# A hybrid block on one core: two feed-forward slices of ten chunks run during the last two chunks, the last chunk's state sums moved from TensorE to GpSimd, B and C computed in column tiles, state copies on ScalarE and state adds on VectorE

## The chip, the cores and the metric

The kernel runs on one core of one Trainium2 chip. The metric is the device time of one execution in microseconds (us), median over the runs. The engines are TensorE (PE, its weight loads PEld), VectorE (DVE), ScalarE (ACT), GpSimd (POOL) and SyncE (SP), which here issues nearly all DMAs.

## The reference, cut to what matters

A block of four residual layers over x of shape (2, 2048, 512), all in float32: an RWKV attention, a feed-forward layer, a Mamba layer and the same feed-forward layer again.

```python
def ffn(x, lut, gate_idx, up_idx, down_idx):       # weights are table entries
    gate = einsum('bsh,oh->bso', x, lut[gate_idx])     # 512 -> 1376
    up   = einsum('bsh,oh->bso', x, lut[up_idx])
    return einsum('bsh,oh->bso', silu(gate) * up, lut[down_idx])   # 1376 -> 512

def mamba(x):                                      # inner width 1024, 16 states
    xs, gate = split(x @ in_proj)                      # 512 -> 2 x 1024
    u = silu(causal_conv4(xs) + conv_b)
    dt_lr, B, C = split(u @ x_proj)                    # 128, 16 and 16 columns
    delta = softplus(dt_lr @ dt_proj + dt_proj_b)
    for t in range(2048):                              # h starts at 0 for each sequence
        h = h * exp(delta[t] * A) + (delta[t] * u[t]) * B[t]     # 1024 x 16 states
        y[t] = sum_n(h * C[t])
    return ((y + u * D) * silu(gate)) @ out_proj

x = x + rwkv(layernorm(x)); x = x + ffn(layernorm(x))
x = x + mamba(layernorm(x)); x = x + ffn(layernorm(x))
```

## The kernel before, in words

The 4096 tokens run in two stages. The first stage (up to about 700 us) is the RWKV layer in eight chunks of 512 tokens. Beside it the 11 slices of feed-forward weights (128 of the 1376 inner columns each, the last has 96) are looked up and written to DRAM as `wff[0..10]`. The second stage does the rest in 16 chunks of 256 tokens, chunks 0 to 7 of one sequence and 8 to 15 of the other.

The second stage is written as a list of steps, each with a time in slots: `line.at(t, fn)` (L52) notes a step, `emit` sorts all steps by time, and the steps are issued in this order. The times therefore only set the order in which each engine's instructions stand. A window has 32 slots, and window `w` starts at `t = 32 * w`. The dictionary `AT` (L538) holds the offsets. In window `w` stand

- the state scan of chunk `w` (`scan`, L819): for each of 2 halves, 4 groups of states `q` and 4 column blocks `c4` POOL computes `du * B` (`grow`, L844) and adds the carried state to the first token (L847); ACT computes the decays (`decay`, L854) for two states at a time into one of three PSUM tiles; DVE runs the scan (L864), multiplies by C (L865) and copies the last token's state to `hst` (L869); POOL adds up the states (`fold`, L876 to L882). That is 32 steps of POOL and 64 of DVE for each chunk;
- the out-projection (`project`) and the second feed-forward layer of chunk `w - 1`, whose result is stored to `out`;
- the front of chunk `w + 1` (`front`, L709): layer norm, in-projection, convolution, and `x_product` (L757), which makes the step sizes and B and C; B and C go to DRAM as `bcd` and come back spread over the partitions (L827);
- the first feed-forward layer of chunk `w + 2`.

So window 14 has no first feed-forward layer, window 15 no front either, and after window 15 only the last chunk's out-projection and second feed-forward layer are left. In the last chunk POOL's `fold` is not used: `spread` (L884) sums the states on PE with matmuls against the identity (L890).

`feed_forward` (L655) takes the slices in pairs, six times `pairs` 0, 2, 4, 6, 8 and the single slice 10: gate and up products (L666), silu on ACT (L684), product on DVE (L693), and at the end the down products of all slices into two PSUM banks (`residual`, L643), which DVE adds to x (L647). The weights come through a `Stream` of 18 buffers of 256 KB, issued by SP in the order of use. PSUM has five banks for all products (`mmp`) and three for the decays (`dap`).

Of the kernel before, what the change touches and what calls it, by code (L numbers as in the profile page):

```python
# [44 lines left out]
class Line:  # L45
# [9 lines left out]
    def emit(self):  # L55
        for _, _, fn, args in sorted(self.items, key=lambda item: item[:2]):
            fn(*args)


@with_exitstack  # L60
def block_kernel(ctx: ExitStack, tc: tile.TileContext, a: dict, out: bass.AP):
# [33 lines left out]
    with ExitStack() as pa:  # L95
# [26 lines left out]
        AA = dict(k=-1.307, r=-0.678, v=-0.887, head=-1.102, sig=-0.532, top=-0.981, e1=-0.692,  # L122
                  e2=-0.655, state=-0.546, vb=-0.433, car=-0.292, num=0.236, den=-0.252, rec=0.174,
                  y=0.611, x=-3.627, stats=-3.064, stat=0.11, each=0.083, copy=0.089, fmul=0.602,
                  opened=-2.211, mean=-2.385, scale=-2.198, turn=-2.092, out=3.908, outs=0.06,
                  add=0.062, looks=(1.565, 14.126), ahead=0.368, load=2.503, cast=1.5, deal=1.4,
                  take=0.479, ff=(14.55, 31.36), place=-8.33, ffln=10.812, nextln=8.791, flast=1.322,
                  turned=1.577, fgate=0.448, fdown=2.092, times=0.273)
# [378 lines left out]
    with ExitStack() as pb:  # L507
        NWS, LEAD = 18, 8.0
        wpool = pb.enter_context(tc.tile_pool(name="b_w", bufs=1))
        xp = pb.enter_context(tc.tile_pool(name="b_x", bufs=8))  # L510
# [16 lines left out]
        wdt = wpool.tile([P, DI], F32, name="wdt")  # L527

        def load_w():
# [8 lines left out]
        AT = dict(total=-0.417, y=1.456, decay=1.1, grow=1.63, fold=2.892, gates=(2.59, 0.82,  # L538
                  24.962, 26.99), front=(6.05, 6.48, 7.41, 8.16), f2=(8.75, 8.93, 12.67, 14.17, 14.38,
                  16.88), f1=(22.279, 21.331, 24.749, 26.059, 30.199, 26.446), f2d=16.9, f1d=30.14,  # L540
                  x=11.293, step0=20.687, step1=10.517, step=0.088, soft=0.09, du=2.158, carry=2.337,
                  zero=3.0, proj=2.49, frontln=3.04, f2ln=5.981, f1ln=18.923, store=29.713, taps=1.14,
                  conv=0.04, unit=1.885, add=0.6, silu=-0.29, hT=0.409, scale=0.19, turn=0.82,
                  g1ln=-4.921, g1=-0.28, g1s=1.491, late=8.031, step1a=-5.78, ahead=12.53, spread=2.23,
                  gsilu=0.359, bca=1.408, step0a=23.69, fronta=(-0.27, 2.4, 1.42, 4.191), xa=14.67)
# [44 lines left out]
        def store_x(ci):  # L590
            for j in range(NJ):
                r = ci * TB + j * P
                nc.sync.dma_start(out[r : r + P, :], xs[ci][j])
            del xs[ci]

        def ln(t, ci, box, to=None):


            def stats():
                box["xnT"] = to if to is not None else tp.tile([P, KC, TB], F32, tag="xnT", name="xnT")  # L600
                st = small.tile([P, NJ, 6], F32, tag="st", name="st")
                mv = small.tile([P, NJ, 2], F32, tag="mv", name="mv")
                rs = small.tile([P, NJ, 1], F32, tag="rs", name="rs")
                for j in range(NJ):
                    V.bn_stats(st[:, j, :], xs[ci][j])  # L605
                    V.bn_aggr(mv[:, j, :], st[:, j, :])
                G.tensor_scalar(rs, mv[:, :, 1:2], EPS, None, ALU.add)
                G.tensor_tensor(rs[:, :, 0], rs[:, :, 0], mhalf[:, :NJ], ALU.pow)  # L608
                nrs = small.tile([P, NJ, 1], F32, tag="nrs", name="nrs")
                G.tensor_scalar(nrs, rs, -1.0, None, ALU.mult)  # L610
                box["mv"], box["rs"], box["nrs"] = mv, rs, nrs

            def scale(j):
                box["xn", j] = wk.tile([P, C], F32, tag="xn", name="xn")
                nm = small.tile([P, 1], F32, tag=f"nm{j}", name="nm")
                S.activation(nm, box["mv"][:, j, 0:1], AF.Copy, scale=box["nrs"][:, j, :])
                S.activation(box["xn", j], xs[ci][j], AF.Identity, bias=nm, scale=box["rs"][:, j, :])  # L617

            def turn(j):
                tr = mmp.tile([P, KC, P], F32, tag="mm", name="tr")  # L620
                for k in range(KC):
                    PE.transpose(tr[:, k, :], box["xn", j][:, k * P : (k + 1) * P], ident)  # L622
                S.copy(box["xnT"][:, :, j * P : (j + 1) * P], tr)  # L623

            line.at(t, stats)
            for j in range(NJ):
                line.at(t + AT["scale"] + 0.1 * j, scale, j)
                line.at(t + AT["turn"] + 0.1 * j, turn, j)

# [25 lines left out]
        def feed_forward(t_ln, times, td, dtd, ci, layer=1):  # L655

            box, hT, ps = {}, {}, {}
            if ci == 1 and layer == 0:
# [39 lines left out]
            for i, ti in zip(range(0, NF, 2), times):  # L698
# [8 lines left out]
            residual([td + dtd * i for i in range(NF)], ci, lambda i: hT[i], lambda i: wff[i][:, 2 * C :])  # L707

        def front(t_ln, times, tx, ci, box):  # L709
# [47 lines left out]
            def x_product():  # L757
                p2 = mm()
                for j, (lo, m) in enumerate(((0, RK), (RK, 2 * NS))):
                    for c in range(ND):  # L760
                        PE.matmul(p2[:m, j, :], lhsT=wxp[:, c, lo : lo + m], rhs=box["u"][:, c, :],
                                  start=(c == 0), stop=(c == ND - 1))
                bcs = wk.tile([2 * NS, TB], F32, tag="bcs", name="bcs", bufs=1)
                S.copy(bcs, p2[: 2 * NS, 1, :])
                box["dtl"] = wk.tile([P, TB], F32, tag="dtl", name="dtl")
                S.copy(box["dtl"], p2[:, 0, :])
# [3 lines left out]
            line.at(tx, x_product)  # L770

# [47 lines left out]
        def scan(t, gates, ci, box):  # L819
# [22 lines left out]
            def grow(half, q, c4):  # L842
# [3 lines left out]
                if ci % (SEQ // TB):  # L846
                    G.tensor_tensor(d[:, :, 0], d[:, :, 0],  # L847
                                    h0[:, 4 * half + c4, 4 * q : 4 * q + 4], ALU.add)
# [8 lines left out]
            def run(half, q, c4, m):  # L857
# [7 lines left out]
                V.tensor_tensor(d[:, two, :], h, cs[half, q][:, two, :], ALU.mult)  # L865
                c, col = 4 * half + c4, 4 * q + 2 * m

                if (ci + 1) % (SEQ // TB):
                    V.tensor_copy(hst[:, c, col : col + 2], h[:, :, TB - 1])  # L869

            def fold(half, q, c4):

                if ci == nchunk - 1:
                    return
# [19 lines left out]
            def total(cp):  # L894

                if ci == nchunk - 1:
                    return
# [5 lines left out]
            def close(cp):  # L903

                if ci == nchunk - 1:
# [9 lines left out]
            for half in range(2):  # L915
# [8 lines left out]
                for q in range(NQ):  # L924
                    line.at(th + 4 * q - 4.0 - AT["bca"] * (ci == 0 and half == 0 and q < 2), load, half, q)
                    for c4 in range(4):
                        s, k = th + 4 * q + c4, (half, q, c4)
                        line.at(s - AT["grow"], grow, *k)
                        for m in range(2):
                            line.at(s - AT["decay"] + 0.5 * m, decay, *k, m)  # L930
                            line.at(s + 0.5 * m, run, *k, m)
                        line.at(s + AT["fold"], fold, *k)
                        if ci == nchunk - 1:
# [10 lines left out]
        for w in range(-1, nchunk + 1):  # L944
            t = SLOTS * w
# [3 lines left out]
            if w > 0:  # L949
# [3 lines left out]
                feed_forward(t + AT["f2ln"], [t + f for f in AT["f2"]], t + AT["f2d"], 0.33, w - 1)  # L953
                line.at(t + AT["store"], store_x, w - 1)
# [13 lines left out]
            if w >= 0 and w + 2 < nchunk:  # L968
                line.at(t + 18.0, load_x, w + 2)
                feed_forward(t + AT["f1ln"], [t + f for f in AT["f1"]], t + AT["f1d"], 0.33, w + 2, layer=0)  # L970
        stream.lay()
# [60 lines left out]
```

## Time and profile before

| | us |
|---|---|
| median of 3 runs | 3535.88 (3534.11 to 3536.36) |
| the profiled execution's own time | 3528.32 |
| its span, first to last instruction | 3526.5 |
| first stage, up to the first scan | 708.5 |
| chunk 0 | 160.2 |
| chunks 1 to 13, each | 171.3 to 173.6 |
| chunk 14, chunk 15 | 165.6, 161.3 |
| after the last scan | 80.9 |

The lower rows are read from the times at which DVE starts the first scan (L864) of each chunk. Busy times overlap where an engine is pipelined, so what counts below is what an engine waits for: a stretch without its waits is what the engine itself needs. A float32 matmul shows as two records.

### The profile page before, as it was taken

What the parts mean: (1) busy time and instruction counts of PE and PEld (TensorE: products, weight loads), DVE (VectorE), ACT (ScalarE), POOL (GpSimd) and SP (SyncE); (2) the same over time, 40 slices, a digit from 0 to 9 for tenths busy, and PEclk for the clock granted to TensorE, in tenths of its full rate; (3) what the DMA queues carried; (4) which work ended last, traced back from release to release, by engine and by line L of the source; (5) the groups of instructions that cost most, each with busy time, mean ns of one, the idle gap of its engine ahead of it and who ended that gap; (6) DMA issues with size and microseconds to landing.
All of it is one profiled execution on the core that took longest, in us unless ns stands there. A gap on an engine that the chain in (4) does not pass through costs nothing. (4 is left out here: it accounts for less than half of the span.)

```text
span 3526.5 us, 45022 instructions
## 1 busy us (share of the span) xinstructions
PE 3355.6 (95%) x13744; PEld 2269.1 (64%) x13744; DVE 2891.1 (82%) x4522; ACT 2575.4 (73%) x4522; POOL 2807.6 (80%) x2755
## 2 busy tenths in 40 slices
PE   7999999889999999999999999999999999998698
PEld 3443555566777777777777777776767676765575
DVE  6777544399989898989898989898989898989882
ACT  6655867578878787878787878787878787877551
POOL 4344434298999999999999998999999999999840
PEclk9999999999999999999999999999999999999899
DMA  6553111365565656565656565656565656563442
GB/s 181 154 157 110 60 54 60 111 231 162 172 210 174 207 179 203 180 201 181 204 176 212 176 209 178 205 180 200 182 204 181 208 179 205 181 200 126 149 141 63
DMA packets 275505, 594.75 MB, mean 169 GB/s; under 512 B 31168, under 2 KB 32832, under 8 KB 275264
## 3 DMA queue, kind: packets, MB, share of 16 engines
q1 hardware_dynamic: 274464, 590.31, 53.4%
q8 instruction: 110, 1.80, 0.2%
q10 hardware_dynamic: 800, 1.57, 0.1%
q14 instruction: 131, 1.07, 0.1%
HBM read 560.96 MB, written 30.80 MB: 168 GB/s over the span
## 5 line engine op out<-in xcount | busy, mean ns | idle before, releaser
L864 DVE TENSOR_TENSOR_SCAN h<-h,db 128x512 f32<-128x512 f32 x1024 | 1252.2, 1223 | 98.5 <-ACT h L854 59.5
L844 POOL TENSOR_TENSOR db<-du,bc 128x1024 f32<-128x1024 f32 x512 | 1206.4, 2356 | 50.9 <-PE y L890 47.9
L854 ACT ACTIVATE h<-dl,acol 128x256 f32<-128x256 f32 x2048 | 952.3, 474 | 288.4 <-DVE hst L869 199.4
L865 DVE TENSOR_TENSOR db<-h,bc 128x512 f32<-128x512 f32 x1024 | 707.7, 691 | 35.9
L876 POOL TENSOR_TENSOR db<-db 128x512 f32<-128x512 f32 x480 | 609.3, 1269 | 0.0
L643 PE MATMUL po<-w,hT 128*128 128x512 f32 x1364 | 602.4, 592 | 0.0
L666 PE MATMUL pg<-xnT,w 128*128 128x256 f32 x2400 | 545.0, 381 | 1.6 <-ACT xnT L623 0.7
L666 PE MATMUL gu<-xnT,w 128*128 128x256 f32 x2400 | 541.0, 380 | 3.5 <-ACT hT L684 3.5
L666 PEld LDWEIGHTS pg<-xnT,w 128*128 128x128 f32 x2400 | 455.4, 191 | 80.4 <-issue 12.5
L666 PEld LDWEIGHTS gu<-xnT,w 128*128 128x128 f32 x2400 | 454.8, 190 | 76.8 <-ACT hT L684 9.1
L643 PEld LDWEIGHTS po<-w,hT 128*128 128x128 f32 x1364 | 258.1, 190 | 282.2 <-issue 266.3
L882 POOL TENSOR_TENSOR acc<-db 128x256 f32<-128x256 f32 x480 | 348.4, 726 | 37.6
L381 PE MATMUL ps<-xnT,wrvk 128*128 128x512 f32 x768 | 344.0, 597 | 0.7 <-ACT xnT L253 0.7
L854 ACT ACT_TABLE_LOAD x246 | 315.6, 1283 | 12.1 <-DVE hst L869 7.5
L381 PEld LDWEIGHTS ps<-xnT,wrvk 128*128 128x128 f32 x768 | 142.4, 190 | 175.6 <-issue 169.5
L834 PE MATMUL ps<-ready,w 128*128 128x256 f32 x1024 | 234.1, 382 | 9.8 <-DMA w<-in_in_proj 9.8
L721 PE MATMUL ps<-ready,w 128*128 128x256 f32 x1024 | 230.4, 384 | 9.2 <-DMA w<-in_in_proj 8.4
L643 PE MATMUL po<-w,u 128*128 128x512 f32 x512 | 229.4, 595 | 3.2 <-DVE u L913 3.2
L834 PEld LDWEIGHTS ps<-ready,w 128*128 128x128 f32 x1024 | 196.7, 192 | 50.6 <-ACT h L854 13.5
L721 PEld LDWEIGHTS ps<-ready,w 128*128 128x128 f32 x1024 | 196.4, 193 | 42.6 <-issue 14.6
L741 DVE SCALAR_TENSOR_TENSOR ps<-xin,cw,ps 128x256 f32<-128x256 f32 x384 | 185.8, 488 | 29.3 <-ACT ps L735 18.8
L443 POOL TENSOR_TENSOR d<-aa,opq 128x512 f32<-128x512 f32 x32 | 39.5, 1236 | 212.6 <-DVE opq L428 155.9
(144 smaller groups left out, 4307.8 us busy)
## 6 DMA issues: line engine op xcount, KB each, us to landing
w<-wff SPq DMA_DIRECT2D x1023, 256.0 KB, 2.7
bc<-bcd SPq DMA_DIRECT2D x256, 512.0 KB, 4.9
w<-in_in_proj SPq DMA_DIRECT2D x256, 256.0 KB, 2.9
w<-in_out_proj SPq DMA_DIRECT2D x128, 256.0 KB, 2.8
ixg<-ixd SPq DMA_DIRECT2D x44, 384.0 KB, 6.2
ix<-in_idx SPq DMA_DIRECT2D x11, 768.0 KB, 9.7
wff<-wt SPq DMA_DIRECT2D x11, 768.0 KB, 4.0
w<-wff SPq DMA_DIRECT2D x11, 768.0 KB, 4.2
```

The lines of the kernel that those rows point to most:

```text
L381: PE.matmul(ps, lhsT=wrvk[:, k, lo : lo + P], rhs=chunk["xnT"][:, k, :], start=(k == 0), stop=(k == KC - 1))
L643: PE.matmul(po[j], lhsT=lw[:, j * P : (j + 1) * P], rhs=w[i]["w"][:m], start=(i == 0), stop=(i == n - 1))
L666: PE.matmul(to[:m], lhsT=w[:, k, :m], rhs=box["xnT"][:, k, :], start=(k == 0), stop=(k == KC - 1))
L721: PE.matmul(ps[cp][:, j, :], lhsT=wj[:, k, :], rhs=box["xnT"][:, k, :], start=(k == 0), stop=(k == KC - 1))
L741: V.scalar_tensor_tensor(ps[cp][:, j, :], xin[cp][:, j, i : i + TB], cw[:, c, i : i + 1], ps[cp][:, j, :], ALU.mult, ALU.add)
L834: PE.matmul(ps[:, j, :], lhsT=wj[:, k, :], rhs=box["xnT"][:, k, :], start=(k == 0), stop=(k == KC - 1))
L844: G.tensor_tensor(d, box["du", half][:, c4, :].unsqueeze(1).to_broadcast([P, 4, TB]), bs[half, q], ALU.mult)
L854: S.activation(h[:, n, :], box["dl", half][:, c4, :], AF.Exp, scale=acol[:, 4 * half + c4, col : col + 1])
L864: V.tensor_tensor_scan(flat(h), flat(h), flat(d[:, two, :]), 0.0, ALU.mult, ALU.add)
L865: V.tensor_tensor(d[:, two, :], h, cs[half, q][:, two, :], ALU.mult)
L876: G.tensor_tensor(d[:, 0:2, :], d[:, 0:2, :], d[:, 2:4, :], ALU.add)
L882: G.tensor_tensor(to, d[:, 0, :], d[:, 1, :], ALU.add)
```

## The change

- **Later slices.** For chunks 2 to 11 (`LATER`) the second feed-forward layer leaves out the pair of slices 8 and 9. The normalised input is written to DRAM (`keep_x`, 512 KB), and x goes to DRAM in place of `out`. Ten steps `rest`, all noted in window 14 with times in windows 14, 15 and 16 (three, six and one), read both back (`fetch_x`), run slices 8 and 9, add, and store to `out`.
- **No identity sums.** `fold`, `total` and `close` test for chunk `nchunk`, which never comes, in place of `nchunk - 1`: the last chunk is summed on POOL like the others.
- **B and C in column tiles.** The eight 32-column products of `x_product` are dealt to four groups of 32 columns, their sum over the four groups is copied from PSUM by ACT, and one matmul with `sum4` (four identities of 32 stacked) adds the groups up (`rates_product`), some 2.8 slots later; only then `bcd` is written.
- **State copies and adds.** The copy to `hst` moves from DVE to ACT (`keep`), 0.27 slots after its scan; the add of the carried state moves from POOL to DVE (`enter`), 0.73 slots ahead of its scan.
- **Order.** `AA` and `AT` have new numbers, and `SHIFT` adds to them in windows -1, 0, 14, 15 and 16. Pools: x tiles 8 to 10, `xnT` 2 to 3.

```diff
-        xp = pb.enter_context(tc.tile_pool(name="b_x", bufs=8))
+        xp = pb.enter_context(tc.tile_pool(name="b_x", bufs=10))
...
+        LATER = range(2, 2 + len(AT["rest"]))
...
+        def keep_x(ci, box):
+            nc.sync.dma_start(xnd[ci], box["xnT"])
+
+        def fetch_x(ci, box):
+            box["xnT"] = tp.tile([P, KC, TB], F32, tag="xnT", name="xnT", bufs=3)
+            nc.sync.dma_start(box["xnT"], xnd[ci])
+            xs[ci] = []
+            for j in range(NJ):
+                x2 = xp.tile([P, C], F32, tag="x", name="x")
+                nc.sync.dma_start(x2, x2d[ci][j * P : (j + 1) * P, :])
+                xs[ci].append(x2)
+
+        def rest(ci, t):
+            box = {}
+            line.at(t - AT["fetch"], fetch_x, ci, box)
+            feed_forward(None, [t], t + AT["restd"], 0.33, ci, pairs=[8], given=box)
+            line.at(t + AT["restd"] + 2.0, store_x, ci)
...
             def x_product():
-                p2 = mm()
-                for j, (lo, m) in enumerate(((0, RK), (RK, 2 * NS))):
-                    for c in range(ND):
-                        PE.matmul(p2[:m, j, :], lhsT=wxp[:, c, lo : lo + m], rhs=box["u"][:, c, :],
-                                  start=(c == 0), stop=(c == ND - 1))
+                p2 = box["p2"] = mm()
+                for c in range(ND):
+                    PE.matmul(p2[:, 0, :], lhsT=wxp[:, c, :RK], rhs=box["u"][:, c, :],
+                              start=(c == 0), stop=(c == ND - 1))
+                for c in range(ND):
+                    g = slice(c % 4 * 2 * NS, (c % 4 + 1) * 2 * NS)
+                    PE.matmul(p2[g, 1, :], lhsT=wxp[:, c, RK:], rhs=box["u"][:, c, :],
+                              start=(c < 4), stop=(c >= 4))
+                parts = box["parts"] = wk.tile([P, TB], F32, tag="parts", name="parts", bufs=1)
+                S.copy(parts, p2[:, 1, :])
+                box["dtl"] = wk.tile([P, TB], F32, tag="dtl", name="dtl")
+                S.copy(box["dtl"], p2[:, 0, :])
+
+            def rates_product():
+                p2 = box["p2"]
+                PE.matmul(p2[: 2 * NS, 1, :], lhsT=sum4, rhs=box["parts"], start=True, stop=True)
                 bcs = wk.tile([2 * NS, TB], F32, tag="bcs", name="bcs", bufs=1)
                 S.copy(bcs, p2[: 2 * NS, 1, :])
...
             line.at(tx, x_product)
+            line.at(tx + AT["rates"], rates_product)
...
-                if ci % (SEQ // TB):
-                    G.tensor_tensor(d[:, :, 0], d[:, :, 0],
-                                    h0[:, 4 * half + c4, 4 * q : 4 * q + 4], ALU.add)
+
+            def enter(half, q, c4):
+                d = db[half, q, c4]
+                V.tensor_tensor(d[:, :, 0], d[:, :, 0],
+                                h0[:, 4 * half + c4, 4 * q : 4 * q + 4], ALU.add)
...
+            def keep(half, q, c4, m):
                 c, col = 4 * half + c4, 4 * q + 2 * m
-
-                if (ci + 1) % (SEQ // TB):
-                    V.tensor_copy(hst[:, c, col : col + 2], h[:, :, TB - 1])
+                S.copy(hst[:, c, col : col + 2], db[half, q, c4, m][:, :, TB - 1])
...
             def fold(half, q, c4):
-                if ci == nchunk - 1:
+                if ci == nchunk:
                     return
...
                         line.at(s - AT["grow"], grow, *k)
+                        if ci % (SEQ // TB):
+                            line.at(s - AT["enter"], enter, *k)
                         for m in range(2):
                             line.at(s - AT["decay"] + 0.5 * m, decay, *k, m)
                             line.at(s + 0.5 * m, run, *k, m)
+                            if (ci + 1) % (SEQ // TB):
+                                line.at(s + 0.5 * m + AT["keep"], keep, *k, m)
...
+                some = w - 1 in LATER
+                pairs = [i for i in range(0, NF, 2) if not (some and i == 8)]
+                box = feed_forward(t + AT["f2ln"], [t + AT["f2"][i // 2] for i in pairs], t + AT["f2d"], 0.33,
+                                   w - 1, pairs=pairs)
+                if some:
+                    line.at(t + AT["f2ln"] + AT["turn"] + 0.4, keep_x, w - 1, box)
+                line.at(t + AT["store"], store_x, w - 1, x2d[w - 1] if some else None)
...
+            if w == nchunk - 2:
+                for ci, r in zip(LATER, AT["rest"]):
+                    rest(ci, t + r)
```

## The prediction

> **What bounds the kernel now.** First the page's busy times, then each engine's waits over chunks 2 to 12, then single stretches.
>
> ```profile
> PE 3355.6 (95%) x13744; PEld 2269.1 (64%) x13744; DVE 2891.1 (82%) x4522; ACT 2575.4 (73%) x4522; POOL 2807.6 (80%) x2755
> ```
>
> PE looks like the bound, but 80% for POOL is a mean with the first stage, where it is half idle. The waits between 1042 and 2945 us (11 chunks), for PE, POOL and the longest of DVE and ACT:
>
> ```profile
> PE ps L761 <- DVE hT L693: 16.2, 11, 1.5
> PE tr L622 <- ACT xn L617: 14.7, 26, 1.0
> POOL rs L607 <- DVE mv L606: 31.3, 13, 5.6
> DVE hT L696 <- PE ps L666: 55.2, 11, 5.5
> ACT h L854 <- DVE hst L869: 129.9, 159, 1.9
> ```
>
> In these 1903 us PE waited 34 us and POOL 33 (3 each per chunk of 173), DVE 147 (13.4 per chunk), ACT 368 (33.5). PE and POOL are both full; relieving PE alone would give 3 us per chunk. The next two views tell what POOL needs without L847: chunks 5, 8, 14 and 15 from the first `grow` on (busy PE, PEld, DVE, ACT, POOL, then clock), and POOL in chunks 7 and 8.
>
> ```profile
> 1556.50:1729.90 173.40, 169.84 (x674) 122.75 (x672) 156.31 (x259) 135.91 (x245) 163.74 (x166) 1.00 0.62 192
> 2075.80:2245.60 169.80, 167.40 (x663) 120.83 (x662) 153.61 (x251) 134.67 (x242) 157.81 (x134) 1.00 0.62 190
> 3112.40:3281.60 169.20, 132.69 (x498) 92.08 (x496) 155.66 (x255) 125.18 (x231) 162.42 (x163) 0.92 0.47 151
> 3281.60:3433.50 151.90, 142.43 (x552) 105.78 (x553) 122.43 (x146) 90.22 (x163) 95.45 (x85) 0.96 0.46 152
> ```
>
> ```profile
> 1799.28 2.35 POOL L844 TENSOR_TENSOR db<-du,bc 128x1024 f32<-128x1024 f32 x1
> 1801.71 0.20 POOL L847 TENSOR_TENSOR db<-db,h 128x4 f32<-128x4 f32 x1
> 1801.86 1.28 POOL L876 TENSOR_TENSOR db<-db 128x512 f32<-128x512 f32 x1
> 1803.21 0.72 POOL L882 TENSOR_TENSOR acc<-db 128x256 f32<-128x256 f32 x1
> 1803.90 2.35 POOL L844 TENSOR_TENSOR db<-du,bc 128x1024 f32<-128x1024 f32 x1
> ...
> 2106.53 2.36 POOL L844 TENSOR_TENSOR db<-du,bc 128x1024 f32<-128x1024 f32 x1
> 2108.84 1.27 POOL L876 TENSOR_TENSOR db<-db 128x512 f32<-128x512 f32 x1
> 2110.20 0.73 POOL L882 TENSOR_TENSOR acc<-db 128x256 f32<-128x256 f32 x1
> 2110.88 2.35 POOL L844 TENSOR_TENSOR db<-du,bc 128x1024 f32<-128x1024 f32 x1
> ```
>
> Chunk 8 starts a sequence and has no L847: one step takes 4.35 us against 4.62. In chunk 14 POOL waited for nothing, though PE had 36 us free: POOL alone sets 169.2 us there. In chunk 15 PE has its identity sums. Last the end, where PE waits for the layer norm:
>
> ```profile
> 3448.06:3455.20 7.14, 7.13 (x16) 2.96 (x16) 2.21 (x4) 0.00 (x0) 0.00 (x0) 1.00 0.33 94
> 3455.20:3460.19 4.99, 0.00 (x0) 0.00 (x0) 2.23 (x5) 1.16 (x3) 1.17 (x3) 0.77 0.22 75
> 3460.19:3463.00 2.81, 2.15 (x8) 1.43 (x8) 0.00 (x0) 2.14 (x5) 0.00 (x0) 0.50 0.00 0
> 3463.00:3467.00 4.00, 3.98 (x9) 3.17 (x10) 0.00 (x0) 1.26 (x1) 0.00 (x0) 0.50 0.00 0
> ```
>
> Five idle us bring the granted clock to 0.50; the transposes take 2.15 us where eight take 1.0 in the first stage, and the first 32 records 9.5 us up to the next group instead of 6.9.
>
> **The change, part by part.** *Later slices.* Records of 256 columns follow each other at 0.216 us, of 512 at 0.430. A pair is 32 gate and up records (6.9 us) and 8 down records (3.4): 10.35 us of PE, 103.5 for ten. ACT loses a silu (0.60) and two table loads (1.28 each), DVE a product (0.7). SP issues six 256 KB loads less and a 512 KB store more; the store waits for ACT's copy of `xnT`, and the weight loads queue behind it. The queue already stands so at L768 (118 us over the 11 chunks, up to 10.8 at once) while 18 buffers hold some 33 us of work, and PE's list shows no wait for weights. Cost nothing; without that cover, up to 10 us per chunk.
>
> *L847 to DVE.* POOL: 32 times 0.27, 8.6 us less per chunk. On DVE the nearest row is L114 (128x4, 0.16 us); followed by something independent such operations pass in 0.07 us, followed by a dependent one in 0.20: 2.2 to 6.4 us, I take 4. It waits for `grow`, with one scan queued behind it, whose own data are ready. POOL's `fold` that uses this scan comes nearly four steps (17 us) later in POOL's order, so nobody late waits for it.
>
> *hst copies to ACT.* DVE's next instruction starts 0.07 us after a copy: 64 copies, 4.5 us less (by the 0.149 of the row, 9.5). On ACT the nearest row is L732 (0.196 us, next start after 0.10): 6.4 to 12.6 us; I take 10. The copy waits for its scan, and queued behind it are the decays for the third tile ahead, which need the same tile's release anyway, and any silu that stands between. Between the two I take the upper half, since a copy that has waited cannot start behind its forerunner at 0.10.
>
> *B and C.* Before: 16 records at 0.216, 3.46 us. In the first stage four records of 32 columns run side by side (24 of L201 in 1.41 us with the change of shape, 0.1). If all four do so here: 0.86 + 0.43 for `sum4` + 0.2 for one more change of shape there and back, 2.0 us less; if none do, 0.6 us more. The two records of one float32 matmul go to the same columns and stand next to each other, so I reckon with two side by side: 0.9 us less. The Trainium skill (TensorE: Matmul & The Clock Gate, Part 3) speaks against the full gain: weight loads overlap running matmuls only in another row group, and three column tiles gave 2.38 times; by that 1.4 us less here. The PSUM bank of `p2` is held 2.8 slots longer, one of five; I take nothing, at worst a pair waits 2 us per chunk.
>
> *No identity sums.* In chunk 15 PE loses 256 records (55 us), POOL gains 32 folds: 32 x (1.34 + 0.68) + 16 x 0.81 = 77.6 us.
>
> *Sum by stage.* POOL in the ten chunks 3 to 12: 173.4 - 2.7 (its wait) - 8.6 = 162.1 us; chunk 8 confirms it with 169.8 less 7.4 of waits, 162.4. PE: 169.8 - 10.35 - 0.9 = 158.6. DVE: 173.4 - 13.4 - 4.5 - 0.7 + 4 = 158.8. ACT: 173.4 - 33.5 - 3.2 + 0.3 + 10 = 147. POOL is the bound; with the loss of 2.9 us that the two full engines show now, 165 us.
> - Chunks 3 to 12: 1729.8 us from first scan to first scan become 1650: -79.8.
> - Chunks 1, 2 and 13 keep PE as bound: 3 x -0.9 = -2.7.
> - Chunk 14: POOL 169.2 - 8.6 = 160.6, PE 132.7 + 3 x 10.35 - 0.9 = 162.8, some of it at the clock of 0.92 that fills up; 163.4: -5.8.
> - Chunk 15: from first `grow` to the last gating, 166.4 us before. POOL: 151.9 - 53.1 idle + 77.6 - 8.6 = 167.8, then one add and the product on DVE, 1.5: +2.9. PE: 142.4 - 55.3 + 62.1 = 149, beside it.
> - End: the pair in the gap. Out-projection to the end of the first 32 records 17.3 us; then 6.9 + 1.0 + 3.4 + 6.9 = 18.2: +0.9, as the clock stays up; +4.8 if it does not.
> - Start of the second stage: twelve weight loads stand on SP between `bcd` and the first B and C (7.3 us, L827 at 699.9), afterwards six, and two more ahead of `bcd`; four less at 0.6 us: -2.4. First stage and chunk 0, reordered: 0, from -8 to +8 (PE waits some 18 us there after its first product).
>
> Together -87: 3526.5 becomes 3439.5. The median stands 9.4 us above that span: 3449.
>
> **Rivals.** *ACT and DVE pace it.* Four engines are left between 147 and 162 us, and DVE waits 4 us per chunk for decays already. If half of DVE's 13.4 us stays, and its waits for decays double by 4 us since ACT stands at copies, the ten chunks take 158.8 + 6.7 + 4 = 170. Then -30 with nothing from the other terms, median 3506. For it: in-order queues bound to each other by three tiles. Against it: PE and POOL, equally full, lose only 3 us.
> *POOL without loss, and retuned order pays*: 162.1, and -8 in the first stage: -29 and -8 more, 3412.
> *Slower: copies hold up ACT.* A copy stands at 0.69 of the space between two decays (0.267 + 1.077 - 1.0 of 0.5 slots), so a third of ACT's some 20 other steps per chunk (silu, softplus, convolution) fall behind one. If each then loses a DVE tile (1.26 + 0.69 us), that is 12 us per chunk behind POOL's 165: 177 in ten chunks (+40), and some 8 more in each of chunks 1, 2, 13, 14 and 15, where PE or POOL hide a third of it (+40): 3616. It decides from about 6 us per chunk on, where 15 chunks lose the 87 again, 9 if DVE's 3 us of slack under POOL take the first part. Against it: ACT waits 12 us per chunk for the same DVE tiles now.
> *Column tiles do not overlap*: +1.5 us in four chunks, hidden by POOL in the ten: 3455, inside the range.
>
> **How the numbers follow.** POOL-bound with a small loss 0.68, paced by ACT and DVE 0.14, without loss 0.08, held up 0.08, all else 0.02. The range reaches to 3414 (no loss) and 3508 (paced), and leaves out the held-up case. A measurement of this kernel can tell about 0.2% from no change (7 us); -87 and -30 are clear of it. Faster 0.90, same 0.02, slower 0.08.
>
> **What would show it.** Right: chunks 3 to 12 take 163 to 167 us between first scans, POOL's waits there stay under 4 us per chunk, PE's grow to 6; L847's successor is short on DVE; chunk 15 has no PE in its sums and POOL full; no clock of 0.50 near the end. Wrong: POOL waiting over 6 us per chunk, DVE's scan waiting on ACT's decays over 8 us, ACT waiting on scans at the copies with silu behind it, PE waiting for weights behind the new store, or the four records of B and C 0.2 us apart.

## The result, and the profile after

The changed kernel takes 3578.51 us (median of four runs, 3577.61 to 3579.03), the kernel before beside it 3534.99: a ratio of 1.0124, with a 95% interval of 1.0107 to 1.0142. The forecast was 3449 us, faster; it was wrong in the sign. The profiled span is 3576.7 us, 50.2 longer than before.

The page's busy line, and from its list of groups the one for the moved add:

```profile
PE 3322.2 (93%) x13520; PEld 2219.5 (62%) x13520; DVE 3101.9 (87%) x4097; ACT 2656.5 (74%) x5406; POOL 2792.9 (78%) x2387
...
L943 DVE TENSOR_TENSOR db<-db,h 128x4 f32<-128x4 f32 x448 | 315.0, 703 | 1.0 <-POOL db L938 0.9
```

DVE issues 425 instructions fewer than before and is busy 211 us longer. The 448 adds of four columns account for more than all of it: 703 ns each on the mean (154 the shortest, 2015 the longest), where POOL took 204 ns and row L114, from which the forecast priced them, 161.

Chunks 5, 14 and 15 from the first `grow` of each on, as the prediction shows them of before (length, then busy PE, PEld, DVE, ACT, POOL, then clock):

```profile
1549.60:1725.70 176.10, 163.05 (x636) 115.16 (x635) 169.64 (x226) 139.17 (x305) 157.65 (x134) 0.98 0.56 182
3127.60:3304.30 176.70, 155.62 (x579) 105.64 (x579) 171.25 (x219) 135.04 (x292) 156.51 (x131) 0.97 0.59 189
3304.30:3469.60 165.30, 146.02 (x518) 100.35 (x518) 159.10 (x198) 114.51 (x199) 150.38 (x120) 0.95 0.68 221
```

The bound has moved: DVE has 169.6 of 176.1 us, POOL 157.7, PE 163. From first scan to first scan chunks 3 to 12 take 175.5 to 176.2, but for chunk 7 (180.0) and chunk 8 (163.7), which starts a sequence and has no adds. The waits over the same 11 chunks say who stands behind DVE:

```profile
ACT hst L965 <- DVE db L961: 208.8, 191, 3.3
POOL rs L686 <- DVE mv L685: 108.0, 32, 7.7
...
PE tr L701 <- ACT xn L696: 49.1, 39, 3.4
...
DVE h L960 <- ACT h L950: 36.3, 32, 2.4
...
POOL db L972 <- DVE db L961: 18.4, 9, 2.0
```

POOL waits for the layer norm's sums (L685) 108 us instead of 31, for these stand in DVE's queue too; in chunk 5 its waits come to 14.2 us (2.7 before) and PE's to 13.0 (3.5). ACT's copies wait 209 us for DVE, on an engine that is not the bound; what the copies cost by themselves is measured below.

Why an add is long shows when DVE's and POOL's lists in order of time (start, duration) are laid side by side, here in chunk 7. First DVE:

```profile
1790.14 0.69 DVE L961 TENSOR_TENSOR db<-h,bc 128x512 f32<-128x512 f32 x1
1790.75 0.91 DVE L943 TENSOR_TENSOR db<-db,h 128x4 f32<-128x4 f32 x1
1791.58 1.22 DVE L960 TENSOR_TENSOR_SCAN h<-h,db 128x512 f32<-128x512 f32 x1
...
1804.87 0.41 DVE L943 TENSOR_TENSOR db<-db,h 128x4 f32<-128x4 f32 x1
...
1809.52 0.15 DVE L943 TENSOR_TENSOR db<-db,h 128x4 f32<-128x4 f32 x1
```

and POOL:

```profile
1789.28 2.35 POOL L938 TENSOR_TENSOR db<-du,bc 128x1024 f32<-128x1024 f32 x1
...
1804.52 0.74 POOL L978 TENSOR_TENSOR acc<-db 128x256 f32<-128x256 f32 x1
...
1808.87 0.73 POOL L978 TENSOR_TENSOR acc<-db 128x256 f32<-128x256 f32 x1
```

The first add ends at 1791.66; POOL's `grow` of another tile ends at 1791.63. The second ends at 1805.28, POOL's L978 at 1805.26. The third begins 0.08 us before the end of POOL's instruction (1809.60) and takes 0.15 us. The list of all 448 says the same:

```profile
L943 DVE TENSOR_TENSOR db<-db,h x448: 154/692/2015, 846.6 to 3483.6; 128x4 f32<-128x4 f32 x150
```

(shortest, median and longest in ns). 59 of them, which met POOL idle or within 0.14 us of the end of an instruction, take at most 163 ns. The other 389 take longer, and each of them ends 19 to 29 ns after the end of an instruction that POOL was running when the add began. These adds show as busy and not as waits: ahead of all 448 DVE waited for POOL's product only 0.9 us in sum.

### The profile page after: what moved, and what is told of

Read it like the earlier page. It is cut to its first block, busy times and chain, and to the rows that moved or that the text cites. A ratio compares the mean times of both kernels' runs of the same rounds, so it can differ in the third digit from the quotient of the medians.

```text
span 3576.7 us, 44353 instructions
## 1 busy us (share of the span) xinstructions
PE 3322.2 (93%) x13520; PEld 2219.5 (62%) x13520; DVE 3101.9 (87%) x4097; ACT 2656.5 (74%) x5406; POOL 2792.9 (78%) x2387
## 3 DMA queue, kind: packets, MB, share of 16 engines
q10 hardware_dynamic: 800, 1.57, 0.1%
## 4 chain that ended last, share of the span: by engine, by line
DVE 45%; PE 28%; ACT 15%; POOL 6%; issue 4%; DMA 2%; SPq 0%; DVEq 0%; ACTq 0%; POOLq 0%
DVE h L960 19%; DVE db L961 9%; PE ps L397 8%; DVE db L943 5%; ACT h L950 4%; DVE ps L825 4%; PE gu L747 3%; PE po L722 3%; PE pg L747 3%; POOL db L938 3%; PE po L370 3%; ACT L950 3%; PE lk L217 2%; DVE y L1008 2%; ACT L765 2%
## 5 line engine op out<-in xcount | busy, mean ns | idle before, releaser
L950 ACT ACTIVATE h<-dl,acol 128x256 f32<-128x256 f32 x2048 | 975.9, 477 | 138.2 <-DVE db L961 78.6
L972 POOL TENSOR_TENSOR db<-db 128x512 f32<-128x512 f32 x512 | 650.2, 1270 | 35.6 <-DVE db L961 27.4
L722 PE MATMUL po<-w,hT 128*128 128x512 f32 (+1 forms) x1364 | 613.4, 602 | 38.7 <-ACT hst L965 19.3
L722 PEld LDWEIGHTS po<-w,hT 128*128 128x128 f32 (+1 forms) x1364 | 261.8, 193 | 342.2 <-issue 278.1
L978 POOL TENSOR_TENSOR acc<-db 128x256 f32<-128x256 f32 x512 | 372.0, 726 | 40.1
L965 ACT COPY hst<-h 128x2 f32<-128x2 f32 x896 | 139.9, 156 | 311.4 <-DVE db L961 310.7
L943 DVE TENSOR_TENSOR db<-db,h 128x4 f32<-128x4 f32 x448 | 315.0, 703 | 1.0 <-POOL db L938 0.9
L928 PE MATMUL ps<-ready,w 128*128 128x256 f32 x1024 | 247.3, 398 | 0.0
L805 PE MATMUL ps<-ready,w 128*128 128x256 f32 x1024 | 231.4, 385 | 11.2 <-DMA w<-in_in_proj 9.5
L928 PEld LDWEIGHTS ps<-ready,w 128*128 128x128 f32 x1024 | 205.8, 202 | 42.8 <-issue 8.9
L805 PEld LDWEIGHTS ps<-ready,w 128*128 128x128 f32 x1024 | 198.1, 194 | 46.3 <-issue 13.6
```

The costliest lines, as they stand in the source:

```text
L722: PE.matmul(po[j], lhsT=lw[:, j * P : (j + 1) * P], rhs=w[i]["w"][:m], start=(i == 0), stop=(i == n - 1))
L805: PE.matmul(ps[cp][:, j, :], lhsT=wj[:, k, :], rhs=box["xnT"][:, k, :], start=(k == 0), stop=(k == KC - 1))
L928: PE.matmul(ps[:, j, :], lhsT=wj[:, k, :], rhs=box["xnT"][:, k, :], start=(k == 0), stop=(k == KC - 1))
L943: V.tensor_tensor(d[:, :, 0], d[:, :, 0], h0[:, 4 * half + c4, 4 * q : 4 * q + 4], ALU.add)
L950: S.activation(h[:, n, :], box["dl", half][:, c4, :], AF.Exp, scale=acol[:, 4 * half + c4, col : col + 1])
L972: G.tensor_tensor(d[:, 0:2, :], d[:, 0:2, :], d[:, 2:4, :], ALU.add)
```

## Experiments

Theory: the add on DVE, with both operands in SBUF, cannot run beside POOL's instruction, and its some 20 us per chunk make DVE the bound. Rivals: the copies on ACT hold DVE up, the later slices' transfers or waits cost the time, or any add at this place of DVE's list does, whatever it reads.

**No add.**

```diff
-                        if ci % (SEQ // TB):
-                            line.at(s - AT["enter"], enter, *k)
```

> The changed kernel without the add of the carried state, on any engine (this leaves out the carry of the state from chunk to chunk). Theory: VectorE loses 20 us per chunk and POOL has no add either, so the sum of the prediction comes into force: POOL 162, chunks 3 to 12 at 164 to 166 us, the kernel 3425 to 3450. Rival (copies on ScalarE): chunks stay above 173, the kernel above 3530. Rival (in-order queues of four nearly full engines lose more): chunks at 168 to 172, the kernel 3470 to 3520.

3396.96 us, ratio 0.9607 [0.9591, 0.9623]: 181.6 us less than the changed kernel, 13 for each of the 14 chunks with adds. Chunks 3 to 12 take 163.8 us on the mean, at the low end of what was expected, and the kernel less than the expected 3425 to 3450. With no engine making the adds, the change brings 138 us; this holds POOL's relief from them as well.

**The add on POOL, right behind its product**, as before, with the rest of the change. (Here the first adds of each second half read the carried state before it is multiplied by its decay.)

```diff
+                if ci % (SEQ // TB):
+                    G.tensor_tensor(d[:, :, 0], d[:, :, 0],
+                                    h0[:, 4 * half + c4, 4 * q : 4 * q + 4], ALU.add)
...
-                        if ci % (SEQ // TB):
-                            line.at(s - AT["enter"], enter, *k)
```

> The changed kernel with one part undone: the carried state is added by POOL again, right behind its product. Theory (VectorE's add reads two SBUF tensors and starts only when POOL's running instruction ends, so 32 adds cost VectorE about 20 us per chunk and make it the bound at 176): VectorE falls to about 155 us busy per chunk, POOL is the bound again with 158 + 4 + 8.6 = 170.6, chunks take 172 to 174, and the kernel 3515 to 3540, about the time of the kernel before. Rival (the copies on ScalarE hold up the decays; in the changed kernel ScalarE waits 310 us at them): chunks stay at 176 and the time above 3560. Rival (a tail and later slices that cost more than they gain): same as before only in the steady chunks, time 3550 or more.

3494.57 us, 0.9879 [0.9864, 0.9893], faster than the expected 3515 to 3540; chunks of 171.0, and POOL's step from `grow` to `grow` 4.62. The same 448 adds cost 98 us on POOL and 182 on DVE.

**Only the add moved, in the kernel before.**

```diff
-                if ci % (SEQ // TB):
-                    G.tensor_tensor(d[:, :, 0], d[:, :, 0],
-                                    h0[:, 4 * half + c4, 4 * q : 4 * q + 4], ALU.add)
+            def enter(half, q, c4):
+                d = db[half, q, c4]
+                V.tensor_tensor(d[:, :, 0], d[:, :, 0],
+                                h0[:, 4 * half + c4, 4 * q : 4 * q + 4], ALU.add)
...
+                        if ci % (SEQ // TB):
+                            line.at(s - 0.726, enter, *k)
```

> The kernel before with one part alone: the add moves to VectorE, 0.726 slots ahead of its scan; nothing else. Theory: VectorE needs 160 us per chunk now, plus about 20 is 180; 13 of the chunks after chunk 0 become 179 to 183 us, the kernel 3600 to 3660, adds between 0.15 us and 2 us long that end just after a POOL instruction ends. Rival (only the combination with the copies on ScalarE or the later slices is slow): POOL falls to 162, PE bounds, chunks stay at 173, the kernel within 0.3% of before.

```profile
L849 DVE TENSOR_TENSOR db<-db,h x448: 132/578/2287, 869.8 to 3626.8; 128x4 f32<-128x4 f32 x150
```

3711.33 us, 1.0494 [1.0478, 1.0510], more than the expected 3600 to 3660. The adds take 774 ns on the mean, and the 379 that take over 170 ns end 18 to 28 ns after POOL's instruction. So neither the copies nor the later slices are needed for the loss. Chunk 8, without adds, takes 172.6 there; the others some 186.

**The same add with an operand in PSUM.** The two instructions stay where they are; the second operand is four columns of a PSUM tile in place of `h0`.

```diff
-                                h0[:, 4 * half + c4, 4 * q : 4 * q + 4], ALU.add)
+                                db[half, q, c4, 0].rearrange("p n t -> p (n t)")[:, :4], ALU.add)
```

> The changed kernel with the add still on VectorE, same place, same 128x4 strided shape, but its second operand is read from PSUM (four columns of the decay tile in place of the carried state, so the state is not carried rightly). Theory (the wait needs two SBUF inputs): every add takes 0.15 to 0.20 us whatever POOL does, chunks 3 to 12 at 164 to 167 us, the kernel 3430 to 3460. Rival (the strided write of one element per state, or any small VectorE instruction beside POOL, is slow): adds stay at 0.7 us on average and the kernel near 3578.

The line's own list (minimum, median and maximum in ns, then what DVE waited for ahead of it):

```profile
L943 DVE TENSOR_TENSOR db<-db,h x448: 149/155/165, 846.5 to 3507.1; 128x4 f32<-128x4 f32 x150
...
  ACT h L950: 192.3, 102
  ACT hst L965: 98.5, 64
```

No add is over 165 ns, though 375 of the 448 began with more than 170 ns of a POOL instruction still to run. The kernel is none the faster for it: 3601.56 us, 1.0185 [1.0170, 1.0200]. The tile chosen was that of the step's own decays, which the add now needs half a step sooner, and DVE waits 290 us for ACT instead. The durations answer the question; the time does not, since the operand brought a wait of its own.

A second try took the tile scanned last, whose data are ready:

```diff
...
+                ran.append(h)
...
-                V.tensor_tensor(d[:, :, 0], d[:, :, 0],
-                                h0[:, 4 * half + c4, 4 * q : 4 * q + 4], ALU.add)
+                V.tensor_tensor(d[:, :, 0], d[:, :, 0], ran[-1].rearrange("p n t -> p (n t)")[:, :4], ALU.add)
```

> As the run with a PSUM operand, but the second operand is four columns of the decay tile that VectorE has just scanned, so the add waits for nothing new on ScalarE (the state is not carried rightly). Before it, the add with a PSUM operand took 0.149 to 0.165 us whatever POOL ran, but it waited for a decay half a step early (192 us). Theory: the adds stay at 0.15 to 0.17 us, chunks 3 to 12 at 164 to 166 us, the kernel 3397 to 3425, some 160 us under the changed kernel. Rival (an add at this place in VectorE's queue costs the time whatever it reads, since it waits for POOL's product with a scan behind it): chunks at 170 or more, the kernel above 3470.

```profile
L943 DVE TENSOR_TENSOR db<-db,h x448: 149/161/165, 846.7 to 3632.0; 128x4 f32<-128x4 f32 x150
...
  ACT hst L965: 375.6, 253
```

Again at most 165 ns, and 3726.80 us (1.0554 [1.0535, 1.0572]). ACT's copy reads the same tile, and DVE's read was put in order behind it, so the time is in the range of the rival but the row names ACT's copy and not POOL's product as what DVE waits for. What the kernel would take with adds of 0.16 us and no such wait on DVE was therefore not measured; the kernel without adds is the nearest to it. Both runs also read another tensor than `h0`; an add with another operand in SBUF was not run.

**The carried state as the scan's start value**, two scans of 256 columns in place of one of 512 and no add at all:

```diff
...
-                V.tensor_tensor_scan(flat(h), flat(h), flat(d[:, two, :]), 0.0, ALU.mult, ALU.add)
+                for n in range(2):
+                    col = 4 * q + 2 * m + n
+                    first = hst[:, 4 * half + c4, col : col + 1] if ci % (SEQ // TB) else 0.0
+                    V.tensor_tensor_scan(h[:, n, :], h[:, n, :], d[:, 2 * m + n, :], first, ALU.mult, ALU.add)
...
```

> A version that carries the state without any add: the changed kernel with 128 scans of 256 in place of 64 of 512 per chunk, each starting from the stored state as its initial value; the steps that prepare the carried state and cut the decays (128 small ScalarE and 96 POOL operations over the kernel) fall away too. Theory: POOL stays at 161 us per chunk, VectorE goes from 155 to 161 to 168 by the fixed part of 64 more scans (0.1 to 0.2 us each, an estimate from 512 elements in 1.22 us), chunks 164 to 170, the kernel 3400 to 3480, under both kernels. Rival (an initial value read from SBUF waits for POOL like the add): scans lengthen to the end of POOL's instruction, chunks above 190, the kernel above 3700.

```profile
L958 DVE TENSOR_TENSOR_SCAN h<-h,hst,db x1792: 726/757/760, 851.8 to 3495.3; 128x256 f32<-128x256 f32 x200
```

3586.56 us, 1.0157 [1.0141, 1.0173], where 3400 to 3480 was expected. A pair keeps DVE 1.57 us up to the next instruction, one scan of 512 keeps it 1.26: 64 times 0.31 is 20 us per chunk, as much as the adds took. The lengths hardly vary beside a busy POOL: one column out of SBUF as start value beside data in SBUF, with the decays in PSUM, is not held up.

**Without later slices**, first with the add on DVE, then without it:

```diff
-        LATER = range(2, 2 + len(AT["rest"]))
+        LATER = range(2, 2)
```

> The changed kernel with one part undone: no slices are left for later, every chunk runs all eleven in its own window. Theory (VectorE sets 176 us per chunk by its adds, PE has 13 us of gaps there): chunks 3 to 12 grow by at most 3 us, 176 to 179, while chunks 14 and 15 and the end get shorter by 15 to 40 us; the kernel 3550 to 3600, that is the later slices bring nothing here. Rival (PE sets the pace in the changed kernel too): chunks grow by 8 to 10 us, the kernel above 3620.

> The changed kernel without the add of the carried state (the state is not carried from chunk to chunk) and without later slices. Beside the run without the add (163.8 us per chunk, 3397) it tells what the later slices bring when VectorE is free. Theory (prediction's sum): PE needs 169 to 170 us per chunk again, chunks 3 to 12 take 170 to 173 us, chunks 14 and 15 and the end get shorter by some 20 to 30 us, the kernel 3430 to 3465. Rival (POOL at 162 sets the pace and PE's slices were hidden): chunks stay at 164 to 166, the kernel below 3400.

3583.61 us (1.0147 [1.0131, 1.0163]) and 3417.38 (0.9676 [0.9659, 0.9693]). Beside 3578.51 and 3396.96, the later slices bring 5 us with DVE as the bound, which the two intervals do not tell from nothing, and 20 with DVE relieved. In the second, chunks take 166.6 us, between what theory and rival expected, and PE is busy for all of a chunk (length, then PE, PEld, DVE, ACT, POOL):

```profile
1532.00:1698.60 166.60, 166.60 (x676) 122.03 (x675) 151.70 (x195) 140.93 (x306) 158.92 (x134) 1.00 0.63 200
```

So PE is the bound without the later slices, and the slices do relieve it.

**Only the copies moved to ACT, in the kernel before.**

```diff
-                if (ci + 1) % (SEQ // TB):
-                    V.tensor_copy(hst[:, c, col : col + 2], h[:, :, TB - 1])
+            def keep(half, q, c4, m):
+                c, col = 4 * half + c4, 4 * q + 2 * m
+                S.copy(hst[:, c, col : col + 2], db[half, q, c4, m][:, :, TB - 1])
...
+                            if (ci + 1) % (SEQ // TB):
+                                line.at(s + 0.5 * m + 0.267, keep, *k, m)
```

> The kernel before with the state copies on ScalarE alone, 0.267 slots after each scan, as in the change. Theory: POOL and PE stay full (171 and 170 us per chunk), VectorE has 4.5 us less to do, ScalarE 10 us more and waits at the copies for scans, which costs nothing: chunks 172 to 174, the kernel within 0.3% of before. Rival (the slower case of the prediction, copies hold up ScalarE's other steps): chunks above 176, the kernel above 3570.

3549.77 us, 1.0044 [1.0029, 1.0059]: 15 us slower, about one per chunk and a little more than the expected 0.3%. Its waits between 1100 and 2900 us have a line that the kernel before lacks:

```profile
DVE h L864 <- ACT hst L869: 36.2, 28, 1.7
```

So the copies do hold DVE up at times, as the third rival of the prediction had it, but at a twelfth of its price of 12 us per chunk. That this line is the whole of the 15 us is not shown.

**Only the order of the first stage** (the changed kernel's `AA` in the kernel before; two of its seven lines):

```diff
-        AA = dict(k=-1.307, r=-0.678, v=-0.887, head=-1.102, sig=-0.532, top=-0.981, e1=-0.692,
+        AA = dict(k=-1.184, r=-0.701, v=-1.026, head=-1.049, sig=-0.304, top=-1.022, e1=-0.731,
...
-                  opened=-2.211, mean=-2.385, scale=-2.198, turn=-2.092, out=3.908, outs=0.06,
+                  opened=-9.346, mean=-2.559, scale=-2.339, turn=-2.075, out=3.831, outs=0.032,
```

> The kernel before with the first stage's order of the changed kernel alone (its AA numbers). In the changed kernel the first scan starts at 690 us, in the one before at 708.5; the prediction had -2.4 there, from the loads ahead of the first scan alone. Theory (the order of the first stage brings it): the first scan starts at 692 to 698 us and the kernel takes 3515 to 3528. Rival (it comes from the second stage's head, the earlier B and C and the loads): first scan at 705 to 709, the kernel within 0.2% of before.

3516.57 us, 0.9948 [0.9931, 0.9964]; its first scan starts at 694.5 us instead of 708.5. Of the 18.6 us by which the changed kernel's first scan is earlier (689.9), the order of the first stage gives 14.0.

**Versions with the add off DVE.** In the first, POOL makes the add as a step of its own, behind an instruction that it does not depend on:

```diff
-                V.tensor_tensor(d[:, :, 0], d[:, :, 0],
+                G.tensor_tensor(d[:, :, 0], d[:, :, 0],
...
-                            line.at(s - AT["enter"], enter, *k)
+                            line.at(s - 0.85, enter, *k)
```

> A version meant to beat both: the changed kernel with the add of the carried state on POOL again, as a step of its own 0.85 slots ahead of the scan, behind the step that prepares the carried state. (In the first run with the add on POOL it stood right behind the product, where the first adds of each second half read the carried state before it was multiplied by its decay.) Theory: POOL needs 162.3 us, as without the add, plus 32 x 0.27 = 171 us per chunk, and chunks take 171 to 173 us; the kernel 3485 to 3505, 0.985 to 0.992 of before.

POOL's list in order of time:

```profile
1803.48 0.20 POOL L943 TENSOR_TENSOR db<-db,h 128x4 f32<-128x4 f32 x1
1803.63 2.36 POOL L938 TENSOR_TENSOR db<-du,bc 128x1024 f32<-128x1024 f32 x1
1805.95 1.28 POOL L972 TENSOR_TENSOR db<-db 128x512 f32<-128x512 f32 x1
1807.30 0.73 POOL L978 TENSOR_TENSOR acc<-db 128x256 f32<-128x256 f32 x1
1807.99 0.20 POOL L943 TENSOR_TENSOR db<-db,h 128x4 f32<-128x4 f32 x1
1808.14 2.36 POOL L938 TENSOR_TENSOR db<-du,bc 128x1024 f32<-128x1024 f32 x1
```

A step is 4.51 us, against 4.35 without an add: from its start to the next instruction an add takes 0.15 us, where right behind its product it cost 0.27. Chunks take 167.1 us, which is 162.3 (POOL without adds) + 32 x 0.15, and not the expected 171 to 173. The kernel takes 3442.08 us, 0.9737 [0.9723, 0.9752]: the fastest of these versions that compute the whole block, 93 us below the kernel before and 136 below the changed one.

The second has POOL compute the first token of a whole group in two small operations and ACT copy it into the tiles:

```diff
+            def entry(half, q):
+                e = start[half, q] = small.tile([P, 4, 4], F32, tag="e0", name="e0")
+                G.tensor_tensor(e, box["du", half][:, :, 0].unsqueeze(2).to_broadcast([P, 4, 4]),
+                                bs[half, q][:, :, 0].unsqueeze(1).to_broadcast([P, 4, 4]), ALU.mult)
+                G.tensor_tensor(e, e, h0[:, 4 * half : 4 * half + 4, 4 * q : 4 * q + 4], ALU.add)
...
+                S.copy(db[half, q, c4][:, :, 0], start[half, q][:, c4, :])
...
```

> Another version meant to beat both: for each group of four states POOL computes the first token's input with the carried state for four column blocks at once (2 operations of 128x16 in place of 4 adds of 128x4), and ScalarE copies four values into each product. Theory: POOL 162.3 + 8 x 2 x 0.25 = 166.3 us per chunk, ScalarE 32 copies of 0.17 us more (5.4 us, it has 20 to spare), no add on VectorE; chunks 167 to 170 us, the kernel 3440 to 3470. Rival (ScalarE now waits for POOL's product 32 times per chunk and holds up decays): chunks above 172, the kernel above 3500.

3466.94 us, 0.9807 [0.9793, 0.9822], as expected, and 25 slower than the plain add on POOL. POOL has 224 small operations instead of 448 and the kernel still loses time. The waits suggest why, which no run tested: ACT's copy waits for POOL's two operations and product (83 us in 1800), DVE's scans wait for these copies (58 us), and POOL waits 29 us for DVE's layer norm sums, where it waited 2.

## Why the prediction was wrong

**The step that failed** is the term "On DVE the nearest row is L114", with its "2.2 to 6.4 us, I take 4" per chunk. L114 and POOL's last instructions ahead of it in the kernel before are

```profile
2.93 0.16 DVE L114 TENSOR_TENSOR wu<-wcol,ucol 128x4 f32<-128x4 f32 x1
1.38 0.88 POOL L144 MEMSET value<- 32x1 f32 x16
```

L114 ran when POOL's last instruction of that stretch had ended, at 2.26; it could show nothing of an add beside POOL. From the first scan on, each large two-tensor instruction of DVE before has one operand in PSUM, so no row there showed the case at all, and the bounds from L114 were no bounds. Measured: an add takes 703 ns on the mean, with the next instruction starting some 0.07 before its end, so 32 x 0.63 = 20 us per chunk. In chunk 5 DVE is busy 151.06 us without adds and 169.64 with them, 18.6 more. The sum for DVE would have read 175 instead of 158.8, with DVE as the bound. "So nobody late waits for it" fell with it: that argument was about the add's wait for `grow`, and the cost was not a wait.

The Trainium skill has a rule for this (SBUF — State Buffer, section "SBUF: two separate sides"): VectorE and GpSimd share a pair of ports under an exclusive lock; a VectorE instruction with two SBUF inputs and a GpSimd instruction that reads SBUF exclude each other for a whole instruction. The traces agree as far as VectorE waiting goes (the long adds end 19 to 29 ns after POOL's instruction; at most 165 ns with one operand in PSUM); none shows POOL held up by an add, for its `grow` takes 2.34 to 2.38 us throughout.

**The rest of the sum** can be read from the kernel without adds and set against its steps. Chunk 5 there, and in the version with the add as POOL's own step (columns as above):

```profile
1511.80:1675.60 163.80, 158.37 (x635) 113.82 (x634) 151.06 (x194) 138.95 (x305) 157.91 (x134) 1.00 0.61 196
```

```profile
1521.30:1688.40 167.10, 158.58 (x636) 113.81 (x635) 151.33 (x193) 139.08 (x305) 162.56 (x166) 1.00 0.60 193
```

| stretch | forecast | without adds | changed kernel |
|---|---|---|---|
| up to the first scan, chunk 0 | -2.4 | -20.8 | -19.2 |
| chunks 1, 2, 13 | -2.7 | -16.7 | +15.6 |
| chunks 3 to 12 | -79.8 | -91.4 | +22.4 |
| chunk 14 | -5.8 | -3.6 | +17.1 |
| chunk 15 and end | +3.8 | +0.6 | +14.3 |
| sum | -87 | -131.9 | +50.2 |

The table is in profiled spans. The forecast put the median 9.4 us above the span, as it stood in the kernel before; in the changed kernel it stands 1.8 above, so some 7 us of the forecast time were the scatter of the kernel before.

- *POOL in chunks 3 to 12.* 162.1 us forecast; chunks are 163.8 and POOL waits 1.5, so 162.3. PE 158.6 forecast, 158.4 measured. The loss of 2.9 us that two full engines show did not carry over: it is 1.5 with one.
- *Copies on ACT.* I took 10 us; the copies pass at some 0.10 us each, the lower end (6.4). By the measure of the forecast, a chunk less its waits, ACT needs 144 in chunk 5 without adds (163.8 - 19.6) where I had 147. DVE's wait for decays, which the rival doubled, was 42 us in 11 chunks before and 36 after; without adds it is 66, and 15 more for the copies, so it did nearly double there, with POOL as the bound.
- *Column tiles.* I took -0.9 us; "if all four do so here" was right. In chunk 0's front the records of four groups and their sum on PE read

```profile
674.49 1.07 PE L848 MATMUL ps<-u,wxp 128*32 128x256 f32 x16
676.37 0.59 PE L857 MATMUL ps<-parts,sum 128*32 128x256 f32 x2 [0.81 <-issue]
```

  16 records pass in 1.07 us, where 16 at 0.216 took 3.46; in chunk 7 four successive records start at 1804.048, .055, .061 and .068. With the sum's 0.59 PE saves 1.8 us by these rows. Four groups give 3.2 times here; the 2.38 for three that the prediction weighs, taken as it stands for four, was too low. Nor did the weight loads need another row group to overlap: in the kernel before, loads over all 128 rows start 2 ns after the start of a record, and from 715 to 716 us PEld is busy for 0.87 us beside PE's 1.00.
- *Chunks 1, 2 and 13.* PE bounds them, as forecast, but they gained 16.7 us and not 2.7. In the kernel without adds and later slices every chunk is of this kind: 166.6 us against 173.4 before, PE's wait of 3.5 gone and its busy time 3.2 lower. Of the 3.2 in chunk 5, counted from record to record, 2.1 are in the products with `wxp` and the sum, 0.5 in the transposes, and the rest is spread over the other groups; why these are shorter was not tested.
- *First stage.* Taken at 0 with -8 to +8, measured -14.0 by itself: the bounds, made from one wait, were too narrow.
- *Chunk 15 and end.* Together +0.6 without adds, where +3.8 was forecast; the border between them moved, since POOL's last folds now begin after the last scan has ended (three without adds, one in the changed kernel). In the changed kernel PE also still has the later pair's records when the scan is over (last scan ends at 3486.9):

```profile
3490.82 7.03 PE L722 MATMUL po<-w,hT 128*128 128x512 f32 x16
3497.68 7.03 PE L722 MATMUL po<-w,u 128*128 128x512 f32 x16
...
3511.45 1.04 PE L701 MATMUL tr<-ident,xn 128*128 128x128 f32 x8
```

  The out-projection (`po<-w,u`) starts 10.8 us after the last scan; in the kernel before it was 2.4. The transposes take 1.04 us instead of 2.15: the clock stays up, as that step said. Without adds and later slices PE stands idle ahead of the out-projection instead, and the transposes take 2.15 again:

```profile
3335.85 5.49 PE L722 MATMUL po<-w,u 128*128 128x512 f32 x8 [48.33 <-DVE u L1009]
...
3350.22 2.15 PE L701 MATMUL tr<-ident,xn 128*128 128x128 f32 x8 [5.00 <-ACT xn L696]
```

- *The rivals.* "ACT and DVE pace it" had the right engine and a wrong price and cause (170 per chunk, from waits; it was 176, from one busy instruction). "Copies hold up ACT" gave nearly the right chunk length for a reason that the runs put at 1 us per chunk. Among the signs of a wrong forecast, "POOL waiting over 6 us per chunk" came (14.2 in chunk 5), and ACT waits at the copies (209 us in the 11 chunks), but none named a DVE instruction grown long.

With the add left out, the kernel falls 17 us below the range's low end; with the add at 20 us per chunk it rises 70 above the high end. The range held neither: at the low end the first stage, chunk 0 and the chunks with PE as bound gave 32 us more than forecast, and the high end took no account of the one price that no row showed.

## What to carry to other kernels

Before an instruction is moved to another engine, look at where its operands lie and who runs beside it in the new place: a price from a row counts only if that row had the same memories and the same neighbour at work. A small instruction whose duration spreads, here from 0.15 to 2 us, may be waiting inside itself; lay its ends against the other engine's ends. When a change mixes several edits, measure the whole without each: here the change is 44 us slower than the kernel before with the adds on DVE, and 93 faster with them on POOL as steps of their own.

## What the runs showed of the hardware

- A DVE add of 128x4 with both operands in SBUF that began beside a POOL instruction with more than 0.14 us to run ended 19 to 29 ns after that instruction (18 to 28 in the kernel before with only the add moved); with one operand in PSUM it took 149 to 165 ns.
- A small POOL instruction costs 0.27 us behind the product that it depends on and 0.15 behind one that it does not.
- Two scans of 256 columns with a start value from SBUF take 1.57 us up to the next instruction, one of 512 takes 1.26.
- Sixteen float32 records of 32 columns pass in 1.07 us in four column groups, and in 3.46 one after the other.
